# Last layer of a sparse graph network: narrow gathered tiles in float16, multiplied into 32 or 64 rows in three bfloat16 parts

## The chip, the cores and the metric

The kernel runs on 1 core of one Trainium2 chip. The metric is the device time of one launch in microseconds (us). Several runs of one kernel are made on the same chip, and their median is what is compared.

## The reference, cut to what matters

Four layers work on `x` (2708 nodes, 512 features, float32) and a matrix `adj` (2708 x 2708). `adj` is sparse: an entry lies at row i and column j with a chance that falls as both numbers grow, so that the first rows and columns are dense and most of the rest is empty; the diagonal is always there. Every layer ends in `x = layernorm(x + layer(x))`. The change concerns the last one only:

```python
bw = sign(weight)
ba = maximum(sign(x), 0.0)
xw = ba @ bw.T              # whole numbers, at most 512 in size
x = layernorm(x + relu(adj @ xw))
```

The entries of `xw` are whole numbers up to 512 in size, which float16 holds exactly. `adj` is float32 with full mantissas.

## The kernel before

**Blocks and tiles.** The function `sparse_layers` does all the work; `dense_layers` is a fallback for an `adj` with more entries than the lists have room for, and isn't run with this input. The 2708 rows are cut into 22 blocks of 128 (the last has 20). Ahead of the layers the kernel lists for each block b the nodes whose column has an entry in its rows, and packs those columns, transposed, into `packed[b]`: tiles of 128 nodes by 128 rows, float32, which stay in SBUF for all layers. `DIRECT` (L34) names the blocks that take column block 0, or 0 and 1, as whole tiles of their own ("direct"); every other tile of a block is gathered, `ROOM[b]` (L31) of them. In blocks 5 to 21, which this change concerns, there are 70 gathered tiles and 14 direct ones. The diagonal stands apart in `dia_own`.

**Narrow tiles.** The lists are sorted so that the first gathered tiles of a block are narrow (`SPLIT` and `SPANS`, L39 to L46): all entries of such a tile's nodes lie in one quarter of the rows (32 rows, four such tiles, blocks marked QQ) or in one half (64 rows, two tiles, HH); QH and HQ have two quarters and a half. Of the 70 tiles 49 are narrow: 28 in the seven QQ blocks 5 to 10 and 12, 12 in the six HH blocks 11, 13, 15, 17, 18 and 20, and 9 in blocks 14, 16 and 19. Layers 0 to 2 use this already: `span(b, i)` (L1326) gives the rows of a tile, `whole_runs` (L1331) groups the tiles that aren't narrow, `narrow_views` (L1343) gives the narrow ones' part of `packed[b]` by width, `in_turns` (L1360) puts the narrow ones last, and `last_of` (L1373) tells which product closes a row range. The last layer of the kernel before doesn't use it: each tile is multiplied into all 128 rows.

**The last layer** (L1984 to the end of `sparse_layers`). The layer before leaves `xw` as float16 rows in DRAM, `xw_rows`, the last product and write at L1929 and L1936. The products take operands in the format F32R, and `halves_of` (L1994) splits an adjacency tile into two such operands: ScalarE casts it to the high part (L1998), VectorE subtracts that to get the low part (L1999), and each tile takes two products that add up in PSUM. `parts` has four such buffers. There are two kinds of blocks:

- Blocks 0 to 4 (`WHOLE3`) are dense and have a PSUM bank each. `whole_tile(j)` (L2060), for j = 0 to 21, loads 128 rows of `xw_rows` (`xs`, L2064), which `widened` (L2004) turns into F32R, and 128 x 640 of the transposed adjacency (`aw`, L2071, 320 KB, four buffers of its own), splits it, and adds ten products (L2075), two to each bank. These blocks can only end once all 22 steps are done.
- Blocks 21 and 5 to 20 (`order3`) are gathered. For each: its own rows (`xo`, L2087) times its diagonal (`dp`, L2095 by ScalarE and L2098 by VectorE, two products, L2103), then two products for each tile (L2114), the tiles in chunks of four (`CH3`). `gather3` (L2048) issues the gathers of a block, one block ahead: `gathered` (L611) has GpSimd fetch 128 rows by a list of node numbers, as F32R, into a pool of 11 buffers (`xg`). Three PSUM banks take turns.

**The order.** Five whole tiles come first (`AHEAD3`), then the gathered blocks, with a whole tile put in after each three gathers due (`FETCHES3`). `finish3` (L2016) closes a block: VectorE takes `relu` and adds x (L2022) and the moments (L2024), two blocks share a reciprocal root (L642 on ScalarE), ScalarE normalises (L2039), and SP's queue writes 128 rows out (L2043). SP's queue also issues the loads of `xs`, `aw` and `xo`. Which instruction comes when on an engine is set ahead of the run by the scheduler of the Tile framework, which reads this program order and its own costs; within an engine the instructions then run in that order, each waiting for its semaphores.

Of the kernel before, what the change touches and what calls it, by code (L numbers as in the profile page):

```python
# [8 lines left out]
F32 = mybir.dt.float32  # L9
F32R = mybir.dt.float32r  # L10
# [9 lines left out]
P = 128  # L20
# [487 lines left out]
def sparse_layers(ctx, tc, x, adj, adj_t, w0_t, b0, w_sa, a_sa, w_gcnb, b_gcnb, wa, ba, wb, bb, w3_t,  # L508
# [19 lines left out]
    def rows(b: int) -> int:  # L528
        return min(P, N - b * P)

    def direct(b: int):

        return tuple(range(NB)) if b == 0 else DIRECT.get(b, ())

    def tiles(b: int) -> int:
        return len(direct(b)) + ROOM[b]
# [71 lines left out]
    def own_by_itself(b: int) -> bool:  # L608
        return b not in direct(b)

    def gathered(pool, dst_w: int, src, b: int, i: int, dtype=F32):  # L611
        t = pool.tile([P, dst_w], dtype, tag="xg", name=f"xg{b}_{i}")
        nc.gpsimd.indirect_dma_start(  # L613
            out=t, out_offset=None, in_=src[:, :],
            in_offset=bass.IndirectOffsetOnAxis(ap=index[b][:, i : i + 1], axis=0),
        )
        return t
# [708 lines left out]
    def span(b: int, i: int):  # L1326

        t, spans = i - len(direct(b)), SPANS[SPLIT[b]]
        return spans[t][1:] if 0 <= t < len(spans) else (0, rows(b))
# [30 lines left out]
    def in_turns(b: int):  # L1360

        nd, n = len(direct(b)), narrow(b)
        mine = list(range(nd, nd + n))
        return [i for i in range(tiles(b)) if i not in mine] + mine
# [8 lines left out]
    def last_of(b: int, i: int, order):  # L1373

        r0, r1 = span(b, i)
        return all(
            span(b, j)[1] <= r0 or span(b, j)[0] >= r1 for j in order[order.index(i) + 1 :]
        )
# [608 lines left out]
    with tc.tile_pool(name="s_l3", bufs=11, reuse_waits="tile") as lp, \  # L1987
            tc.tile_pool(name="s_ps_w", bufs=1, reuse_waits="tile", space=PSUM) as ps_w, \
            tc.tile_pool(name="s_ps_3", bufs=3, reuse_waits="tile", space=PSUM) as ps_3:
        W3 = WHOLE3 * P  # L1990
        CH3 = 4
        PW = max(CH3 * P, W3)

        def halves_of(a, r: int, w: int, name: str):  # L1994

            p = lp.tile([P, 2, PW], F32R, tag="parts", name=f"p{name}", bufs=4)
            low, high = p[:r, 0, :w], p[:r, 1, :w]
            nc.scalar.copy(high, a)  # L1998
            nc.vector.tensor_tensor(low, a, high.bitcast(F32), op=ALU.subtract)  # L1999
            return p  # L2000

        turn = [0]

        def widened(t, r: int, name: str, tag: str = "wide", bufs: int = 4):  # L2004

            g = lp.tile([P, D], F32R, tag=tag, name=f"w{name}", bufs=bufs)
            turn[0] += 1
            if turn[0] % 3 == 0:
                nc.vector.tensor_copy(g[:r], t[:r])
            else:  # L2010
                nc.scalar.copy(g[:r], t[:r])
            return g

        moments = []

        def finish3(b: int, ps, more: bool):  # L2016

            m = rows(b)
            old = place_of_x(b)
            k = len(moments)  # L2020
            t = old[:, :D]
            nc.vector.scalar_tensor_tensor(t[:m], ps[:m], 0.0, t[:m], op0=ALU.max, op1=ALU.add)  # L2022
            st = small.tile([P, 6], F32, tag="st", name=f"st_3_{b}")
            nc.vector.bn_stats(st[:m], t[:m])  # L2024
            mv = moments[0][2] if k else lp.tile([P, 2, 2], F32, tag="mv3", name=f"mv_3_{b}", bufs=3)
            nc.vector.bn_aggr(mv[:m, k, :], st[:m])
            moments.append((b, t, mv))
            if more:
                return
            n = len(moments)  # L2030
            rs = lp.tile([P, 2, 2], F32, tag="rs3", name=f"rs_3_{b}", bufs=2)
            mean, v = mv[:m, :n, 0], mv[:m, :n, 1]
            nc.vector.tensor_scalar(v, v, LN_EPS, None, op0=ALU.add)
            rsqrt_of(rs[:m, 0, :n], v, m, n, f"3_{b}")
            nc.vector.scalar_tensor_tensor(
                rs[:m, 1, :n], mean, -1.0, rs[:m, 0, :n], op0=ALU.mult, op1=ALU.mult
            )
            for k, (b, t, _) in enumerate(moments):
                nc.scalar.activation(  # L2039
                    t[:m], t[:m], AF.Identity, bias=rs[:m, 1, k : k + 1],  # L2040
                    scale=rs[:m, 0, k : k + 1],
                )
                nc.sync.dma_start(out[b * P : b * P + m, :], t[:m])  # L2043
            moments.clear()

        sources3 = {}

        def gather3(b: int):  # L2048
            sources3[b] = [gathered(lp, D, xw_rows, b, t, F32R) for t in range(ROOM[b])]

        order3 = [NB - 1, *range(WHOLE3, NB - 1)]
        gather3(order3[0])
        gather3(order3[1])


        whole = [ps_w.tile([P, D], F32, tag=f"w{b}", name=f"l3_{b}") for b in range(WHOLE3)]

        xw_direct = {0: xw0}

        def whole_tile(j: int):  # L2060
            r = rows(j)
            if j:
                g = lp.tile([P, D], F16, tag="xs", name=f"xs{j}", bufs=4)
                nc.sync.dma_start(g[:r], xw_rows[j * P : j * P + r, :])  # L2064
                g = widened(g, r, f"s{j}", "wide" if j > 1 else "wide1", 4 if j > 1 else 1)
                if j == 1:
                    xw_direct[1] = g
            else:
                g = xw0
            a = lp.tile([P, W3], F32, tag="aw", name=f"aw{j}", bufs=4)  # L2070
            nc.sync.dma_start(a[:r], adj_t[j * P : j * P + r, :W3])  # L2071
            p = halves_of(a[:r], r, W3, f"w{j}")
            for b in range(WHOLE3):
                for h in range(2):
                    nc.tensor.matmul(  # L2075
                        whole[b], p[:r, h, b * P : (b + 1) * P], g[:r, :],
                        start=(j == 0 and h == 0), stop=(j == NB - 1 and h == 1),
                    )
        j = 0
        while j < AHEAD3:  # L2080
            whole_tile(j)
            j += 1
        due = 0
        for at, b in enumerate(order3):
            m = rows(b)
            xo = lp.tile([P, D], F16, tag="xo", name=f"xo{b}", bufs=2)
            nc.sync.dma_start(xo[:m], xw_rows[b * P : b * P + m, :])  # L2087
            xo = widened(xo, m, f"o{b}")
            if at + 1 < len(order3) and at:
                gather3(order3[at + 1])  # L2090
            src = [xw_direct[j] for j in direct(b)] + sources3.pop(b)
            ps = ps_3.tile([P, D], F32, tag="mm", name=f"l3_{b}")

            dp = lp.tile([P, 2, P], F32R, tag="dp", name=f"dp{b}", bufs=2)
            nc.scalar.activation(  # L2095
                dp[:m, 1, :m], ident[:m, :m], AF.Copy, scale=dia_own[:m, b : b + 1]
            )
            nc.vector.scalar_tensor_tensor(  # L2098
                dp[:m, 0, :m], ident[:m, :m], dia_own[:m, b : b + 1],
                dp[:m, 1, :m].bitcast(F32), op0=ALU.mult, op1=ALU.subtract,  # L2100
            )
            for h in range(2):
                nc.tensor.matmul(  # L2103
                    ps[:m], dp[:m, h, :m], xo[:m, :], start=(h == 0), stop=False
                )
            for i0 in range(0, tiles(b), CH3):
                n = min(CH3, tiles(b) - i0)
                p = halves_of(
                    packed[b][:, i0 : i0 + n, :].rearrange("p n i -> p (n i)"), P, n * m,
                    f"{b}_{i0}",  # L2110
                )
                for i in range(n):
                    for h in range(2):
                        nc.tensor.matmul(  # L2114
                            ps[:m], p[:, h, i * m : (i + 1) * m], src[i0 + i],
                            start=False, stop=(i0 + i == len(src) - 1 and h == 1),
                        )
            pending = bool(moments)
            finish3(b, ps, not pending and b not in (order3[0], order3[-1]))
            if j == NB and whole and len(moments) == 1:  # L2120
                finish3(WHOLE3 - len(whole), whole.pop(0), False)
            due += ROOM[b]
            while j < NB and due >= FETCHES3:
                whole_tile(j)
                j += 1
                due -= FETCHES3
        while whole:
            finish3(WHOLE3 - len(whole), whole.pop(0), len(whole) % 2 == 1)
# [77 lines left out]
```

## Time and profile before

| | |
|---|---|
| Median of three runs | 1006.92 us (1006.87 to 1007.9) |
| Own time of the profiled execution | 1015.66 us |
| Its span | 1013.9 us, 12803 instructions |
| Granted TensorE clock, mean | 0.924 |
| Busy: PE, DVE, ACT, POOL | 867.5, 654.6, 381.2, 513.0 us |
| All transfers | 220.06 MB, mean 217 GB/s |
| Gathers of the whole kernel (queue q0) | 127.61 MB, 42.1% of 16 DMA engines |
| Gathers of the last layer (from 887 us on) | 18.35 MB in 10080 packets |

PE is TensorE's matrix product and PEld its load of weights, which lies beside it; DVE is VectorE, ACT ScalarE, POOL GpSimd, SP the engine whose queue issues most plain transfers. A group of instructions in the profile has its code line, its engine and operation, output<-input by name, shape and count, then its busy time, the mean of one in nanoseconds, and the idle time of the engine ahead of it with what ended most of it. A row of the table of stretches has start and end, length, then the busy time and count of each engine, the granted TensorE clock, the share of the 16 DMA engines that was busy (packets that overlap count each, so it can pass 1) and the GB/s. A row of the chain of waits has the time at which a piece began, its length, and what it was. Averages over the whole kernel say little here: the last layer is one eighth of the span.

### The profile page before, as it was taken

To read this page: it belongs to the slowest core of one execution; us is meant where nothing else is said; L and a number is where in the kernel's file an instruction comes from. 1 tells how busy PE (TensorE), PEld (TensorE's weight loads), DVE (VectorE), ACT (ScalarE), POOL (GpSimd) and SP (SyncE) were. 2 spreads that over 40 slices of the span, in tenths; PEclk is the share of its full clock that TensorE was granted. 3 is DMA by queue.
4 is the path that set the end of the run, shared out by engine and by line. 5 is a ranking of instruction groups with operands and counts; after the bars stand their busy time and mean duration, and the time that the engine had idled before them with its cause. 6 is when DMAs were issued, how large, how long until landed. Compare 5 with 4: busy or idle time off the path is not lost.

```text
span 1013.9 us, 12803 instructions
## 1 busy us (share of the span) xinstructions
PE 867.5 (86%) x3659; PEld 458.7 (45%) x3659; DVE 654.6 (65%) x2538; ACT 381.2 (38%) x822; POOL 513.0 (51%) x579
## 2 busy tenths in 40 slices
PE   1888889659587977989999988998999999699983
PEld 0444444212122324455555544453555555378762
DVE  5889797717366863546455436666888777556765
ACT  2665555100000012545445433333444333254654
POOL 2677888567666533646434034453454320066761
PEclk9898889879798988999999998999999999889986
DMA  9999895467676634766645266676786551299985
GB/s 288 332 330 313 293 299 162 142 197 215 189 228 202 199 122 132 216 198 207 199 150 165 80 235 239 225 272 219 261 320 224 176 176 44 82 308 331 310 233 169
DMA packets 93557, 220.06 MB, mean 217 GB/s; under 512 B 13660, under 2 KB 28364, under 8 KB 93476
## 3 DMA queue, kind: packets, MB, share of 16 engines
q0 software_dynamic: 43008, 127.61, 42.1%
q1 hardware_dynamic: 38520, 76.78, 22.3%
q10 hardware_dynamic: 11948, 14.76, 4.4%
q8 instruction: 31, 0.51, 0.2%
q14 instruction: 50, 0.41, 0.1%
HBM read 178.21 MB, written 31.71 MB: 207 GB/s over the span
## 4 chain that ended last, share of the span: by engine, by line
PE 63%; DVE 15%; issue 6%; DMA 6%; another core or an unknown queue 5%; ACT 3%; POOL 1%; ACTq 0%; DVEq 0%; SPq 0%; POOLq 0%
PE l L1369 11%; PE h L1595 7%; PE e L1820 6%; PE a L1820 6%; PE l L2075 4%; PE y L1106 4%; PE pg L1868 4%; PE l L2114 3%; PE pc L1868 3%; DMA xg<-x_rows,i 2%; PE e L1628 2%; PE px L1929 2%; PE a L1629 2%; DVE s_mask L874 1%
## 5 line engine op out<-in xcount | busy, mean ns | idle before, releaser
L613 POOL DMA_INDIRECT xg<-x_rows,i x98 | 94.8, 967 | 113.4 <-PE l L1369 65.7
L1072 POOL DMA_INDIRECT a<-in_adj_t_dram,row_at x98 | 111.0, 1132 | 59.2 <-DVE deg L817 24.0
L613 POOL DMA_INDIRECT xg<-y_rows,i x98 | 97.5, 995 | 50.3 <-issue 21.8
L1106 PE MATMUL y<-s_w,xt 128*128 128x512 f32 (+1 forms) x176 | 96.8, 702 | 0.0
L1369 PE MATMUL l<-xg,a 128*32 128x512 f32 (+3 forms) x196 | 83.2, 657 | 12.1 <-DMA xg<-y_rows,i 11.8
L613 POOL DMA_INDIRECT xg<-xw_rows,i x70 | 71.4, 1020 | 39.9 <-issue 16.5
L1796 POOL DMA_INDIRECT xg<-x_rows,i x60 | 59.9, 999 | 61.8 <-ACT ae L1551 18.0
L1595 PE MATMUL h<-s_wsa,xt 128*128 128x256 f32 (+3 forms) x352 | 83.5, 391 | 5.2 <-ACT xt L1590 5.0
L1796 POOL DMA_INDIRECT a<-x_rows,i x38 | 36.9, 970 | 93.3 <-DVE mask L1554 38.0
L1595 PEld LDWEIGHTS h<-s_wsa,xt 128*128 128x128 f32 (+1 forms) x352 | 65.4, 190 | 30.6 <-ACT xt L1590 14.0
L809 ACT ACTIVATE unused<-arow 128x1408 uint8<-128x1408 f32 (+3 forms) x44 | 58.3, 1325 | 2.4 <-DMA x_rows<-s_zero 1.7
L1106 PEld LDWEIGHTS y<-s_w,xt 128*128 128x128 f32 (+1 forms) x176 | 37.3, 223 | 43.4 <-issue 43.3
L2075 PE MATMUL l<-ws,pw 128*128 128x512 f32 (+1 forms) x210 | 52.0, 401 | 3.7 <-DVE pw L1999 3.7
L1820 PE MATMUL a<-xg,a 128*32 128x512 f32 (+2 forms) x120 | 50.9, 626 | 4.2 <-DMA xg<-x_rows,i 4.2
L1820 PE MATMUL e<-xg,ae 128*32 128x512 f32 (+2 forms) x120 | 47.9, 601 | 0.9 <-ACT ae L1556 0.9
L642 ACT ACTIVATE rsqs<-mv 128x1 f32<-128x1 f32 (+2 forms) x56 | 11.3, 201 | 94.8 <-DVE mv L671 48.9
L2075 PEld LDWEIGHTS l<-ws,pw 128*128 128x128 f32 (+1 forms) x210 | 40.4, 194 | 14.0 <-DVE pw L1999 4.6
L1868 PE MATMUL pg<-s_wg,pt 128*128 128x256 f32 (+1 forms) x176 | 44.9, 397 | 1.3 <-ACT pt L1856 1.3
L895 PE MATMUL find<-s_sides,s_mask 128*128 128x5 bf16 (+1 forms) x462 | 15.7, 166 | 34.8 <-DVE s_mask L891 25.0
L667 DVE BATCH_NORM_STATS2 st<-t 128x6 f32<-128x512 f32 (+1 forms) x66 | 45.3, 686 | 0.3
L1369 PEld LDWEIGHTS l<-xg,a 128*32 128x32 f32 (+3 forms) x196 | 19.6, 148 | 53.2 <-issue 33.0
L673 POOL TENSOR_TENSOR rs<-mv,s_neg_half 128x1 f32<-128x1 f32 (+1 forms) x22 | 12.9, 588 | 60.5 <-DVE mv L671 51.1
(306 smaller groups left out, 1965.6 us busy)
## 6 DMA issues: line engine op xcount, KB each, us to landing
arow<-in_adj_dram SPq DMA_DIRECT2D x21, 704.0 KB
arow<-in_adj_dram SPq DMA_DIRECT2D x21, 650.0 KB
x_rows<-f SPq DMA_DIRECT2D x40, 256.0 KB
aw<-in_adj_t_dram SPq DMA_DIRECT2D x21, 320.0 KB
y_rows<-yt ACTq DMA_DIRECT2D x20, 256.0 KB
x_rows<-h SPq DMA_DIRECT2D x19, 257.0 KB
f<-in_x_dram SPq DMA_DIRECT2D x19, 256.0 KB
h_own<-x_rows SPq DMA_DIRECT2D x19, 256.0 KB
```

The costliest lines, as they stand in the source:

```text
L613: nc.gpsimd.indirect_dma_start(out=t, out_offset=None, in_=src[:, :], in_offset=bass.IndirectOffsetOnAxis(ap=index[b][:, i : i + 1], axis=0),)
L667: nc.vector.bn_stats(st[:m], t[:m])
L809: nc.scalar.activation(unused[:m, : ar.shape[1]], ar, AF.Copy, accum_out=row_sums[:m, b, h : h + 1])
L1072: nc.gpsimd.indirect_dma_start(out=packed[b][:, t + len(direct(b)), :], out_offset=None, in_=adj_t, in_offset=bass.IndirectOffsetOnAxis(ap ...
L1106: nc.tensor.matmul(ps[:m], xt[:, k, :m], w0[:, k, :], start=(k == 0), stop=(k == KC - 1))
L1369: nc.tensor.matmul(ps[r0:r1], weights, moving, start=(i == order[0]), stop=last_of(b, i, order))
L1595: nc.tensor.matmul(ps, xt[:, k, :m], w[:, k, :], start=(k == 0), stop=(k == KC - 1))
L1796: nc.gpsimd.indirect_dma_start(out=g, out_offset=None, in_=x2_rows[:, :], in_offset=bass.IndirectOffsetOnAxis(ap=index[b][:, t : t + 1], a ...
L1820: nc.tensor.matmul(ps[r0:r1], weights, moving, start=(i == order[0]), stop=last_of(b, i, order))
L1868: nc.tensor.matmul(ps, pt[:, k, :m], w[:, k, :], start=(k == 0), stop=(k == KC - 1))
L2075: nc.tensor.matmul(whole[b], p[:r, h, b * P : (b + 1) * P], g[:r, :], start=(j == 0 and h == 0), stop=(j == NB - 1 and h == 1),)
L2114: nc.tensor.matmul(ps[:m], p[:, h, i * m : (i + 1) * m], src[i0 + i], start=False, stop=(i0 + i == len(src) - 1 and h == 1),)
```

## The change

The narrow tiles of the last layer are treated as such, as in the layers before:

- `gather3` fetches a narrow tile's 128 rows as float16, as they lie in DRAM, into buffers of their own (`xh`, 12), and a whole tile's as F32R as before (`xg`, 8); of one block the whole tiles are fetched first, the narrow ones last.
- To make room, the tiles of adjacency streamed for blocks 0 to 4 (`aw`) have no buffers of their own: they take turns in four slices of `packed[1]`, `packed[2]` and `packed[3]`, which the last layer doesn't read.
- Whole tiles are split in two and multiplied as before, but in the runs that `whole_runs` gives.
- A narrow block's part of the adjacency is split in three bfloat16 parts (`thirds`, two buffers, with the float32 rest in `left`, one buffer): ScalarE copies the high part of the block's 32- or 64-row pieces, VectorE subtracts it, ScalarE copies the middle part, VectorE subtracts again. Where a block has quarters and a half (14, 16, 19), the first two steps are made once for each width.
- Each narrow tile then takes three products, high part first, each into its own 32 or 64 rows of the block's PSUM bank: all tiles of the block with one part, then with the next.

```diff
--- before.py
+++ after.py
@@ -608,8 +608,8 @@
     def own_by_itself(b: int) -> bool:
         return b not in direct(b)
 
-    def gathered(pool, dst_w: int, src, b: int, i: int, dtype=F32):
-        t = pool.tile([P, dst_w], dtype, tag="xg", name=f"xg{b}_{i}")
+    def gathered(pool, dst_w: int, src, b: int, i: int, dtype=F32, tag="xg", bufs=None):
+        t = pool.tile([P, dst_w], dtype, tag=tag, name=f"{tag}{b}_{i}", bufs=bufs)
         nc.gpsimd.indirect_dma_start(
             out=t, out_offset=None, in_=src[:, :],
             in_offset=bass.IndirectOffsetOnAxis(ap=index[b][:, i : i + 1], axis=0),
@@ -2046,7 +2046,14 @@
         sources3 = {}
 
         def gather3(b: int):
-            sources3[b] = [gathered(lp, D, xw_rows, b, t, F32R) for t in range(ROOM[b])]
+            nd = len(direct(b))
+            sources3[b] = {
+                i: gathered(
+                    lp, D, xw_rows, b, i - nd, *((F16, "xh", 12) if span(b, i) != (0, rows(b))
+                    else (F32R, "xg", 8)),
+                )
+                for i in in_turns(b) if i >= nd
+            }
 
         order3 = [NB - 1, *range(WHOLE3, NB - 1)]
         gather3(order3[0])
@@ -2056,6 +2063,11 @@
         whole = [ps_w.tile([P, D], F32, tag=f"w{b}", name=f"l3_{b}") for b in range(WHOLE3)]
 
         xw_direct = {0: xw0}
+
+        streamed = [
+            packed[b].rearrange("p n i -> p (n i)")[:, k * W3 : (k + 1) * W3]
+            for b, k in ((1, 0), (2, 0), (1, 1), (3, 0))
+        ]
 
         def whole_tile(j: int):
             r = rows(j)
@@ -2067,7 +2079,7 @@
                     xw_direct[1] = g
             else:
                 g = xw0
-            a = lp.tile([P, W3], F32, tag="aw", name=f"aw{j}", bufs=4)
+            a = streamed[j % 4]
             nc.sync.dma_start(a[:r], adj_t[j * P : j * P + r, :W3])
             p = halves_of(a[:r], r, W3, f"w{j}")
             for b in range(WHOLE3):
@@ -2088,7 +2100,9 @@
             xo = widened(xo, m, f"o{b}")
             if at + 1 < len(order3) and at:
                 gather3(order3[at + 1])
-            src = [xw_direct[j] for j in direct(b)] + sources3.pop(b)
+            src = sources3.pop(b)
+            src.update((i, xw_direct[c]) for i, c in enumerate(direct(b)))
+            order_ = in_turns(b)
             ps = ps_3.tile([P, D], F32, tag="mm", name=f"l3_{b}")
 
             dp = lp.tile([P, 2, P], F32R, tag="dp", name=f"dp{b}", bufs=2)
@@ -2103,8 +2117,7 @@
                 nc.tensor.matmul(
                     ps[:m], dp[:m, h, :m], xo[:m, :], start=(h == 0), stop=False
                 )
-            for i0 in range(0, tiles(b), CH3):
-                n = min(CH3, tiles(b) - i0)
+            for i0, n in whole_runs(b, CH3):
                 p = halves_of(
                     packed[b][:, i0 : i0 + n, :].rearrange("p n i -> p (n i)"), P, n * m,
                     f"{b}_{i0}",
@@ -2113,7 +2126,28 @@
                     for h in range(2):
                         nc.tensor.matmul(
                             ps[:m], p[:, h, i * m : (i + 1) * m], src[i0 + i],
-                            start=False, stop=(i0 + i == len(src) - 1 and h == 1),
+                            start=False, stop=h == 1 and last_of(b, i0 + i, order_),
+                        )
+            if narrow(b):
+                p = lp.tile([P, 3, P], BF16, tag="thirds", name=f"p{b}_n", bufs=2)
+                left = lp.tile([P, P], F32, tag="left", name=f"r{b}", bufs=1)
+                mine = []
+                for i0, r0, w, a in narrow_views(b):
+                    n = a.shape[1]
+                    nc.scalar.copy(p[:, 2, r0 : r0 + n * w].rearrange("p (n i) -> p n i", n=n), a)
+                    nc.vector.tensor_tensor(
+                        left[:, r0 : r0 + n * w].rearrange("p (n i) -> p n i", n=n), a,
+                        p[:, 2, r0 : r0 + n * w].rearrange("p (n i) -> p n i", n=n),
+                        op=ALU.subtract,
+                    )
+                    mine += range(i0, i0 + n)
+                nc.scalar.copy(p[:, 1, :], left)
+                nc.vector.tensor_tensor(p[:, 0, :], left, p[:, 1, :], op=ALU.subtract)
+                for h in (2, 1, 0):
+                    for i in mine:
+                        r0, r1 = span(b, i)
+                        nc.tensor.matmul(
+                            ps[r0:r1], p[:, h, r0:r1], src[i], start=False, stop=h == 0
                         )
             pending = bool(moments)
             finish3(b, ps, not pending and b not in (order3[0], order3[-1]))
```

In the changed file the lines are: gathers L613 as before, `streamed` L2067, loads of `xs` L2076, of `aw` L2083 and of `xo` L2099, products of whole tiles of blocks 0 to 4 L2087, of the diagonal L2117, of gathered whole tiles L2127; the narrow blocks' four steps L2137 (ACT), L2138 (DVE), L2144 (ACT), L2145 (DVE), and their products L2149.

## The prediction

> **What bounds the kernel now.** I read the page's 40 slices first, then the last layer alone: its groups of instructions, its busy time by stretch, and the chain of waits. The layer runs from the first gather at 889.05 us to the end of the span. Its groups:
>
> ```profile
> L613 POOL DMA_INDIRECT xg<-xw_rows,i x70 | 71.4, 1020 | 39.9 <-issue 16.5 <-PE l L2114 8.4 <-DMA xw_rows<-xw 7.6
> L2075 PE MATMUL l<-ws,pw 128*128 128x512 f32 (+1 forms) x210 | 52.0, 401 | 3.7 <-DVE pw L1999 3.7
> L2114 PE MATMUL l<-xg,p 128*128 128x512 f32 (+1 forms) x140 | 37.3, 412 | 0.0
> ```
>
> The gathered products (L2114) take 37.3 us of TensorE, and GpSimd waited 8.4 us for them to free gather buffers. The stretches (start and end, length, then busy PE, PEld, DVE, ACT, POOL, then granted clock and DMA share):
>
> ```profile
> 889.00:903.00 14.00, 13.98 (x51) 11.04 (x52) 4.83 (x8) 4.62 (x9) 10.65 (x11) 0.83 1.19 344
> 903.00:969.30 66.30, 65.80 (x286) 52.82 (x284) 45.17 (x116) 38.55 (x76) 46.39 (x45) 1.00 1.10 316
> 969.30:981.80 12.50, 9.29 (x33) 6.93 (x33) 9.17 (x24) 7.27 (x15) 7.48 (x8) 0.86 0.77 216
> 981.80:1002.10 20.30, 16.10 (x55) 12.14 (x54) 15.33 (x59) 10.56 (x21) 6.88 (x8) 0.77 0.66 197
> 1002.10:1013.90 11.80, 0.00 (x0) 0.00 (x0) 4.34 (x20) 2.75 (x6) 0.00 (x0) 0.50 0.38 141
> ```
>
> Until 969.3 TensorE is the bound, with the DMA engines also full (share over 1, as packets overlap). Then it starves once. 981.8 is the end of the last whole tile (L2075), after which five waiting blocks can be finished; the 20.3 us from there to the last matmul belong mostly to VectorE (15.3 busy). The chain says where TensorE starved:
>
> ```profile
> 966.49 4.39 issue
> 970.87 0.73 ACT pw L1998
> 971.63 0.84 DVE pw L1999
> 972.51 4.05 PE l L2075 x10
> ```
>
> "issue" ahead of the cast of an adjacency tile means that ScalarE waited for something the profile doesn't show; with the DMA full I read it as the tile's late load. TensorE then restarts at a low clock: 4.05 us for ten products that take 2.27 in the chain at 944.69. So a product of 128x512 costs 0.227 us.
>
> **What the Trainium skill says.** "TensorEngine Tiling (Array Packing)", Tiling Modes: 32-column weights make four independent tiles, 64-column ones two, and changing the mode drains the array. The trace agrees for float32 in layer 1:
>
> ```profile
> 498.64 0.82 PE L1595 MATMUL h<-s_wsa,xt 128*128 128x260 f32 x3
> 499.39 1.07 PE L1369 MATMUL l<-xg,incn 128*32 128x512 f32 x8
> 500.38 0.70 PE L1628 MATMUL e<-h,e 128*128 128x512 f32 x1
> ```
>
> Eight passes over four 32-row tiles fit before 500.38, while full tiles need 0.86 us for two passes (483.29 to 484.15): four run side by side. The next full product starts 0.13 us after 499.39 + 0.86; where a narrow one follows a full one (535.47 + 0.86, then 536.42) it is 0.09. I price a change of mode at 0.11. "TensorE: Matmul & The Clock Gate", Measured speedup vs the span model, gives 2.38x for three column tiles, less than this trace; that is my lower bound. Its Back-to-back issue gap gives 215.7 ns for 512 columns; the bfloat16 px products here (L1929) take 0.86 for four, 0.215. "DMA: Bandwidth & Descriptors", SWDGE vs HWDGE vs iDMA, says a float32r destination always casts. In the trace a float16 row does land as 2 KB: 18.35 MB in 70 gathers is 128 rows of 2 KB each.
>
> **The change part by part.** The built program shows the order on each engine; durations are from the trace.
>
> 1. Narrow products. 49 of the 70 gathered tiles are narrow. Gone: 98 products x 0.227 = 22.2 us. Added: blocks of one width (7 of four tiles, 6 of two) need 3 rounds each, the three mixed ones (14, 16, 19) 6, since 32 and 64 columns alternate: (39 + 18) x 0.227 = 12.9. Changes of mode: 13 x 2 + 3 x 7 = 47, x 0.11 = 5.2. TensorE net: -4.1. What counts is the part before the last whole tile, blocks 5 to 15: 37 tiles, 74 x 0.227 = 16.8 gone, 36 rounds = 8.2 and 27 changes = 3.0 added: -5.6. After it, 5.4 gone and 4.8 + 2.2 added: +1.6 on TensorE, beside a VectorE that is slower there; 0 on the path, 1.6 without that cover. Bounds of the overlap: all of it (this), 2.38 of 4 (0.38 us a round of four, +3.2 before the last whole tile), none (rival B).
> 2. Start. The two dp steps (0.31 and 0.40 before the cast at 887.40) stand behind the first cast now: -0.65.
> 3. Streamed tiles in the place of blocks 1 to 3. The first four loads move ahead of SP's h_own loads of blocks 19 and 20. They wait for the last reads of block 18's rows (the product at 841.61); h_own 19 waits for u at 843.09 anyway and is used at 855.07. Cost 0; uncovered, 11 us of slack would have to go first. The load itself (1.3 MB) falls where no gather is in flight (830 to 889). Later loads still wait only for their own reader, four back.
> 4. DMA. A 2-KB packet takes 108 ns (queue q0: 53.5% of 16 engines over 126.9 us, 10080 packets); the 1-KB rows written by queue q10 take 42 ns. I take 54, half (bounds 42 and 108). 35 narrow gathers fall before 970: each saves 128 x 54 ns / 16 = 0.43, in all 15 of the 89.6 share-us up to 969.3 (14.0 x 1.19 + 66.3 x 1.10). That is 17%, more than TensorE's speed-up of 5.6 in 92, so I take the starvation as gone: 3.2 of wait (969.3 to 972.5) and 1.8 of slow clock, -5.0. Bound: 0, if the wait isn't the DMA's.
> 5. Gathers. 20 buffers end GpSimd's 12 us of waits for TensorE, but the order moves: xg of later blocks goes ahead, and block 8's last narrow gather becomes the 26th. At 1.245 us each (0.94 + 0.30) it is issued at 889.05 + 25 x 1.245 + 0.94 = 921.1; with about 2 us to land (an estimate from the fixed cost that the same DMA page gives under Anatomy of one DMA; no run here shows it), 923.1, against a need near 922: +1, between 0 and 2.4 (mean pace 1.32). The 70th lands at 978 to 984, before TensorE needs it.
> 6. Preparation. Casts and subtractions of whole tiles: 20 of 128 columns (0.29), 7 of 256 (0.40 on ScalarE, 0.41 on VectorE), one small: 8.8 us on each engine. Narrow ones: 35 steps x 0.29 = 10.1 on each. Against 14.4 (ACT) and 15.6 (DVE) now: +4.5 and +3.3. Beside TensorE, which has the longer queue; but a narrow block is a chain of four steps over two engines (1.2 us), with one `left` and two `thirds` buffers, and behind it in both queues stand casts of streamed tiles. I book +1 (0 to 4).
> 7. The tail. 20.3 us from last whole tile to last matmul, set by VectorE, and 11.8 after it: unchanged (17 to 22 for the first).
>
> Sum: -5.6 - 0.65 - 5.0 + 1 + 1 = -9.2 us. The profiled execution's own time is 1015.66 (span 1013.9 and 1.8 around it), 8.7 above the median of the runs, 1006.92; scaling by their ratio changes the 9.2 by 0.1, so I subtract it: 997.7.
>
> **Rivals.**
> A. Preparation or late loads keep TensorE waiting: the wait at 969 stays (-5.0 lost) and the chain of step 6 costs 2 more: -9.2 + 5.0 + 2 = -2.2, 1004.7. For it: VectorE and ScalarE gain work. Against: 45.2 and 38.6 busy of 66.3.
> B. Slower: 16-bit narrow products do not run side by side. 111 products x 0.227 + 3.0 - 16.8 = +11.4 before the last whole tile, -0.65 - 5.0 + 2: +7.8, 1014.7. It decides from 0.157 us a product ((16.8 - 3.0 + 5.65 - 2) / 111), fewer than 1.45 side by side. Against it: float32 shows four.
> C. The tail shrinks too: VectorE waited 4.7 us there for products (L2022 on L2114), and nothing of steps 5 and 6 shows: 17 for 20.3, -9.2 - 3.3 - 2 = -14.5, 992.4.
> D. It does not do what it says: the saved TensorE time lies in the shadow of the gathers (70 x 1.32 = 92 us) and nothing changes: 1006.9.
>
> **Numbers.** Forecast 0.47, A 0.22, C 0.20, B 0.07, D 0.04. A measurement of this kernel tells 0.2% (2 us) from no change. Faster: 0.47 + 0.20 + nearly all of A = 0.87; same 0.05; slower 0.08. Range 989.5 to 1005: from 3 below C (tail at its lower bound, casts cheaper) to A; it leaves out B, D and some of A.
>
> **What would show it.** Step 1: narrow groups of 128*32 with twelve products in about 0.7 us. Step 4: DMA share below 1.0 from 903 on, no gap ahead of a streamed cast near the end. Step 5: GpSimd without waits for PE, last gather by 982. Steps 1 to 6 together: last whole tile near 972.6; step 7: 20 us from there to the last matmul. I am wrong if rounds take over 0.4 us, or if TensorE waits for thirds or casts by more than 3 us in all.

## The result and the profile after

The changed kernel took 1019.26 us (median of six runs, 1017.22 to 1029.47), the kernel before on the same chip 1007.63. The ratio is 1.0118, with a 95% interval of 1.0084 to 1.0153: slower by 1.2%, where 0.9% faster was forecast, and outside the range. A ratio is worked out from the single runs, without those in a slower state of the chip, and so need not be the quotient of the medians. The profiled execution took 1018.41 us, span 1016.1.

The first layers ended earlier in this profile than in the one of before (last write of `xw_rows` issued at 879.16 against 886.41), so only the last layer is compared, counted from that write. Until the end of the span it took 137.0 us against 127.5.

Groups of the last layer, to be held against L2075 and L2114 of before:

```profile
L2087 PE MATMUL l<-ws,pw 128*128 128x512 f32 (+1 forms) x210 | 57.4, 428 | 14.3 <-issue 10.3 <-DVE rsqs L661 2.3 <-DVE pw L1999 1.7
L613 POOL DMA_INDIRECT xh<-xw_rows,i x49 | 49.1, 1003 | 23.8 <-issue 11.3 <-remote 3.6 <-PE l L2149 3.5
...
L2149 PE MATMUL l<-xh,p_n 128*32 128x512 f16 (+1 forms) x147 | 17.9, 386 | 1.7 <-ACT p_n L2144 1.6
...
L2022 DVE SCALAR_TENSOR_TENSOR f<-l,f 128x512 f32<-128x512 f32 (+1 forms) x20 | 13.7, 689 | 21.0 <-remote 10.1 <-PE l L2127 3.6 <-PE l L2149 3.2
```

TensorE idled 14.3 us ahead of products of streamed tiles, 3.7 before. VectorE waited 10.1 us in the first step of `finish3` for a signal ("remote") that the profile can't pin to an instruction that ended just then. A signal is an update of a semaphore, by which one engine tells the others that an instruction of its own is done. The stretches:

```profile
881.40:898.70 17.30, 17.23 (x74) 12.61 (x74) 6.16 (x15) 6.65 (x17) 13.10 (x13) 0.88 0.91 279
898.70:912.70 14.00, 7.38 (x20) 5.46 (x20) 4.01 (x9) 3.92 (x8) 8.50 (x9) 0.76 0.73 206
912.70:986.20 73.50, 64.64 (x314) 43.93 (x312) 47.86 (x153) 42.24 (x104) 48.15 (x49) 0.95 0.74 223
986.20:1004.10 17.90, 14.88 (x66) 7.12 (x66) 15.32 (x65) 10.11 (x28) 0.00 (x0) 1.00 0.29 107
```

The DMA share fell from 1.10 to about 0.74, as forecast, and bought nothing. In the second row everything stands half idle: 7.4 us of TensorE, 4 of VectorE and ScalarE in 14 us. The timeline of TensorE there, then of VectorE (start, length, and in brackets the idle time before):

```profile
897.85 0.83 PE L2149 MATMUL l<-xh,p_n 128*32 128x512 f16 x12
903.98 5.93 PE L2087 MATMUL l<-ws,pw 128*128 128x512 f32 x14 [5.30 <-issue]
910.93 0.39 PE L2087 MATMUL l<-ws,pw 128*128 128x512 f32 x1 [1.01 <-issue]
```

```profile
902.52 0.68 DVE L2022 SCALAR_TENSOR_TENSOR f<-l,f 20x512 f32<-20x512 f32 x1 [2.39 <-remote]
903.12 0.80 DVE L1999 TENSOR_TENSOR pw<-a,pw 128x640 fp32r<-128x640 f32 x1
...
911.94 0.69 DVE L2022 SCALAR_TENSOR_TENSOR f<-l,f 128x512 f32<-128x512 f32 x1 [6.60 <-remote]
```

The `f` at 911.94 is block 5's; in the built program it waits for TensorE alone, for block 5's last narrow product. That product ended at 898.7, so its signal came 13 us late. The `f` at 902.52 is block 21's, whose last product ended at 896.1: 6 us late. In VectorE's queue the subtraction of the next streamed tile (903.12) stands behind it, and TensorE waits for that from 898.7 to 903.98. Then it runs fourteen products in 5.93 us, at half clock.

The kernel before had this too. In its trace the updates of TensorE's semaphore have times: 85 of the 663 that were recorded came more than 0.6 us after any product that makes one had ended, and one of them, at 970.81, is what released the cast at 970.87: before it, the trace has no update of that semaphore after 961.58, though TensorE ended products up to 969.26. The cast's wait covers two semaphores, TensorE's and that of its own load, and the load, issued at 948.95, had its last packet at 953.77. The "issue" before that cast, which the prediction read as a late load, was a late signal.

### The profile page after: what moved, and what is told of

Same layout as the page of the kernel before. It is cut to its first block, busy times and chain, and to the rows that moved or that the text cites. A ratio compares the mean times of both kernels' runs of the same rounds, so it can differ in the third digit from the quotient of the medians.

```text
span 1016.1 us, 12953 instructions
## 1 busy us (share of the span) xinstructions
PE 860.2 (85%) x3708; PEld 442.5 (44%) x3708; DVE 652.3 (64%) x2571; ACT 383.5 (38%) x855; POOL 512.2 (50%) x579
## 4 chain that ended last, share of the span: by engine, by line
PE 61%; DVE 14%; issue 7%; DMA 6%; another core or an unknown queue 4%; ACT 3%; POOL 3%; ACTq 0%; DVEq 0%; SPq 0%; POOLq 0%
PE l L1369 12%; PE h L1595 7%; PE e L1820 6%; PE a L1820 6%; PE l L2087 5%; PE pg L1868 3%; PE y L1106 3%; PE pc L1868 3%; POOL xg L613 2%; DMA xg<-x_rows,i 2%; PE e L1628 2%; DVE s_mask L874 2%; PE a L1629 2%; PE l L1430 2%
## 5 line engine op out<-in xcount | busy, mean ns | idle before, releaser
L613 POOL DMA_INDIRECT xg<-x_rows,i x98 | 94.8, 968 | 109.6 <-PE l L1369 62.2
L613 POOL DMA_INDIRECT xg<-y_rows,i x98 | 98.7, 1007 | 45.5 <-issue 22.5
L1106 PE MATMUL y<-s_w,xt 128*128 128x512 f32 (+1 forms) x176 | 92.4, 674 | 1.8 <-ACT xt L1098 1.8
L1796 POOL DMA_INDIRECT xg<-x_rows,i x60 | 59.7, 995 | 63.0 <-ACT ae L1551 17.7
L2087 PE MATMUL l<-ws,pw 128*128 128x512 f32 (+1 forms) x210 | 57.4, 428 | 14.3 <-issue 10.3
L613 POOL DMA_INDIRECT xh<-xw_rows,i x49 | 49.1, 1003 | 23.8 <-issue 11.3
L2087 PEld LDWEIGHTS l<-ws,pw 128*128 128x128 f32 (+1 forms) x210 | 42.3, 206 | 29.0 <-issue 13.5
L1369 PEld LDWEIGHTS l<-xg,a 128*32 128x32 f32 (+3 forms) x196 | 20.3, 150 | 55.8 <-issue 35.9
L874 DVE TENSOR_SCALAR s_mask<-arow 128x1408 bf16<-128x1408 f32 (+3 forms) x42 | 39.6, 942 | 5.6 <-DMA arow<-in_adj_dram 5.6
```

Source lines behind the costliest of these rows:

```text
L613: nc.gpsimd.indirect_dma_start(out=t, out_offset=None, in_=src[:, :], in_offset=bass.IndirectOffsetOnAxis(ap=index[b][:, i : i + 1], axis=0),)
L874: nc.vector.tensor_scalar(mask[:m, c0 : c0 + ar.shape[1]], ar, 0.0, None, op0=ALU.not_equal)
L1106: nc.tensor.matmul(ps[:m], xt[:, k, :m], w0[:, k, :], start=(k == 0), stop=(k == KC - 1))
L1369: nc.tensor.matmul(ps[r0:r1], weights, moving, start=(i == order[0]), stop=last_of(b, i, order))
L1796: nc.gpsimd.indirect_dma_start(out=g, out_offset=None, in_=x2_rows[:, :], in_offset=bass.IndirectOffsetOnAxis(ap=index[b][:, t : t + 1], a ...
L2087: nc.tensor.matmul(whole[b], p[:r, h, b * P : (b + 1) * P], g[:r, :], start=(j == 0 and h == 0), stop=(j == NB - 1 and h == 1),)
```

## The experiments

There were six sets of runs: the recorded one and five more, each set on one chip together with the kernel before. They found two levels, and the trace tells them apart:

| | Chip number on record | Kernel before, median | Late updates of TensorE's semaphore, before or nearest kernel |
|---|---|---|---|
| Recorded runs | none | 1007.63 | 85 of 663 in the trace (796 were due) |
| Set 1 | 7 | 1010.73 | 88 of 663 (room18) |
| Set 2 | 15 | 960.12 | 3 of 796 (again) |
| Set 3 | 9 | 960.56 | 3 of 809 (changed) |
| Set 4 | 1 | 1020.15 | 135 of 680 (onering2) |
| Set 5 | 7 | 959.97 | 3 of 801 (stream11b) |

So the signals are late and partly missing in the trace at one level, prompt and complete at the other, and the kernel before is 47 to 60 us faster where they are prompt. That they make up the whole of this difference isn't shown: the last layer's part of it is 9.3 us in the profiles (127.5 against 118.2 in `again`). Nor is it known what makes them late. Sets 1 and 5 have the same chip number and different levels, so, if the number stands for one piece, it isn't the chip alone; whether the taking of the trace has a part no run here can tell. The ratios against before, with their intervals:

| Kernel | Late signals | Prompt signals |
|---|---|---|
| changed | 1.0118 [1.0084, 1.0153] | 1.0024 [1.0009, 1.0039] |
| slices alone (not run with late signals) | | 0.9994 [0.9971, 1.0017]; 0.9999 [0.9977, 1.0020] |
| slices, 18 buffers | 1.0094 [1.0057, 1.0131] | 0.9992 [0.9974, 1.0010] |
| apart | 1.0141 [1.0088, 1.0194] | |
| plain32 | 1.0073 [1.0040, 1.0107] | |
| halves16 | 1.0105 [1.0061, 1.0149] | |
| ownaw | | 1.0047 [1.0029, 1.0066] |
| few | | 1.0024 [1.0005, 1.0043]; 1.0042 [1.0026, 1.0057] |
| onering | 1.0068 [1.0044, 1.0092] | 0.9952 [0.9930, 0.9974] |
| ring16 | 1.0012 [0.9980, 1.0043] | |
| ringplain | 1.0020 [0.9989, 1.0051] | |
| all16 (not run with late signals) | | 0.9934 [0.9908, 0.9959]; 0.9930 [0.9912, 0.9949] |

The theories before set 1, in the letters of the expectations: P, the narrow tiles' preparation keeps TensorE waiting; S, its signals are late because narrow products come in dense bursts; B, the slices or the new buffers cost. From set 2 on, S stands for the slices alone and G for gathers that run ahead and crowd other loads; from set 3 on, O for the order of gathers and L for late signals.

**Set 1: one part alone, and less preparation.** `room18` is the kernel before with the slices and 18 buffers:

```diff
-    with tc.tile_pool(name="s_l3", bufs=11, reuse_waits="tile") as lp, \
+    with tc.tile_pool(name="s_l3", bufs=18, reuse_waits="tile") as lp, \
...
+        streamed = [
+            packed[b].rearrange("p n i -> p (n i)")[:, k * W3 : (k + 1) * W3]
+            for b, k in ((1, 0), (2, 0), (1, 1), (3, 0))
+        ]
...
-            a = lp.tile([P, W3], F32, tag="aw", name=f"aw{j}", bufs=4)
+            a = streamed[j % 4]
```

> The kernel before with the buffers alone changed: streamed adjacency tiles in the slices of packed[1..3], 18 gather buffers for 11, all tiles still whole, F32R, in the old order of gathers. Theory P (the narrow blocks' four steps of preparation and the ring of `parts` keep TensorE waiting): same as before within 0.3%, or up to 4 us faster, since GpSimd waits less. Theory S (TensorE's completion signals come late because narrow products are issued in dense bursts): the same, 1003 to 1008. Theory B (it is the streamed slices or the new buffers): slower than before by 5 us or more, 1012 to 1019.

Measured 1018.10, the loss that theory B expected, without one narrow tile.

`apart` is the changed kernel with the split parts of the gathered blocks' whole tiles in buffers apart (`own` is true for these):

```diff
-            p = lp.tile([P, 2, PW], F32R, tag="parts", name=f"p{name}", bufs=4)
+            own = w < W3
+            p = lp.tile(
+                [P, 2, 2 * P if own else W3], F32R, tag="few" if own else "parts",
+                name=f"p{name}", bufs=3 if own else 4,
+            )
```

> The changed kernel, with the split parts of gathered whole tiles in three buffers of their own (256 columns), so that the four `parts` buffers belong to the streamed tiles alone and their casts can run further ahead. Theory P: 4 to 10 us faster than the changed kernel, 1009 to 1015. Theories S and B: within 2 us of it, 1017 to 1021.

Measured 1021.97: no gain, so sharing the ring of `parts` isn't the cause.

`plain32` multiplies narrow tiles in float32, gathered as float32 into 9 buffers, without any preparation (the lines that fall away aren't shown):

```diff
-                    lp, D, xw_rows, b, i - nd, *((F16, "xh", 12) if span(b, i) != (0, rows(b))
+                    lp, D, xw_rows, b, i - nd, *((F32, "xh", 9) if span(b, i) != (0, rows(b))
...
+                for i in range(len(direct(b)), len(direct(b)) + narrow(b)):
+                    r0, r1 = span(b, i)
+                    nc.tensor.matmul(
+                        ps[r0:r1], packed[b][:, i, r0:r1], src[i], start=False, stop=True
+                    )
```

> The changed kernel, with the narrow tiles multiplied in plain float32 straight from packed[b] (two passes in one instruction, as layer 1 does) on rows gathered as float32: no thirds, no left, none of the four steps on ScalarE and VectorE; 9 narrow buffers for 12. TensorE has about 0.2 us more for a QQ block, and gathered rows land as 2 KB again. Theory P: most of the loss is gone, 1004 to 1011. Theory S: the bursts stay, 1016 to 1021. Theory B: 1017 or more, as the packets are larger too.

Measured 1019.75, where theories S and B expected it and P didn't; its runs spread from 1011.82 to 1029.71.

`halves16` uses two float16 parts:

```diff
-                p = lp.tile([P, 3, P], BF16, tag="thirds", name=f"p{b}_n", bufs=2)
+                p = lp.tile([P, 2, P], F16, tag="halves", name=f"p{b}_n", bufs=4)
...
-                for h in (2, 1, 0):
+                for h in (1, 0):
```

> The changed kernel, with two float16 parts for three bfloat16 ones of each narrow tile: two steps of preparation for four, two rounds of products for three, four buffers for the parts. Theory P: half of the loss or more is gone, 1005 to 1013. Theory S: bursts are shorter (8 for 12 products), 1013 to 1018. Theory B: 1016 to 1019, TensorE's saved rounds at most.

Measured 1019.09. Theory P (preparation) had expected gains of 4 us or more from all of the last three. The changed kernel itself wasn't in this set; against its recorded ratio of 1.0118 theirs are 1.0141, 1.0073 and 1.0105, and all the intervals overlap. P in that size fell, S didn't fit `room18`, and theory B was left.

**Set 2: which half of theory B.** `stream11` is `room18` with 11 buffers.

> The kernel before with one edit: streamed adjacency tiles in the slices of packed[1..3]; 11 gather buffers, whole tiles, F32R. Theory S (the streamed slices cost: their first loads go ahead of others on SP's queue, and the casts come in another order): slower than before by 5 to 10 us. Theory G (gathers that run ahead of TensorE crowd the loads of streamed tiles and own rows): within 2 us of before.

`ownaw` is the changed kernel with `aw` in its own buffers and 9 `xh`.

> The changed kernel with the streamed tiles in four buffers of their own again; to make room, 9 narrow gather buffers for 12. Theory S: most of the loss is gone, 1000 to 1010. Theory G: 17 buffers let the gathers run ahead as before, 1015 to 1020.

`few` is the changed kernel with 5 `xg` and 6 `xh` buffers.

> The changed kernel with 5 buffers for whole gathered tiles and 6 for narrow ones, 11 in all as in the kernel before; streamed slices as changed. Theory S: no gain, 1016 to 1021. Theory G: GpSimd is held back again and the loss is mostly gone, 1005 to 1011.

`again` is the kernel before.

> The kernel before, unchanged, for a second profile of it and for the spread of its own times. Every theory: the same time; from the last write of xw_rows to the end of the span some 127 us, as in the first profile, with one gap of TensorE before the last whole tile.

Measured 961.10, 965.38, 963.78 and 960.54 against 960.12. The slices cost nothing here, so theory S fell for this level, and `ownaw` kept a loss without them. `few` kept one too, with 11 buffers, so theory G found no support. But the level was new, so that the times expected can't be held against these, and `again` showed why; its groups and its stretch up to the last whole tile:

```profile
L2075 PE MATMUL l<-ws,pw 128*128 128x512 f32 (+1 forms) x210 | 49.7, 390 | 0.0
...
L2114 PE MATMUL l<-xg,p 128*128 128x512 f32 (+1 forms) x140 | 35.9, 401 | 0.0
```

```profile
842.50:928.40 85.90, 85.90 (x369) 69.51 (x369) 60.01 (x148) 51.72 (x100) 63.41 (x63) 0.98 1.16 331
```

TensorE doesn't wait at all, with the DMA share even higher, at 1.16. The expectation of one gap was wrong: with prompt signals there is no starvation to cure.

**Set 3: the changed kernel with prompt signals, and its gathers put in order.** `changed` is the changed kernel.

> The changed kernel once more, unaltered, because the chips so far differ in level (the kernel before took 1007 to 1011 us on the first, 960 us on the second, where TensorE's completion signals were hardly ever late). Theory O (two rings of buffers let the whole gathered tiles of later blocks overtake the narrow ones, and TensorE waits near block 8) and theory L (late signals on some chips, which hit the changed kernel more): slower than before by 0.2 to 0.6% where signals are prompt, with a wait of 3 to 6 us on a narrow gather near the 23rd to 26th; slower by 1.0 to 1.4% where they are late. If it is slower by 1% with prompt signals, both fall.

Measured 962.28 against 960.56, and the wait was where theory O put it. TensorE and then GpSimd near block 8:

```profile
878.32 0.39 PE L2149 MATMUL l<-xh,p_n 128*32 128x512 f16 x1
879.57 0.38 PE L2149 MATMUL l<-xh,p_n 128*32 128x512 f16 x1 [0.86 <-DMA xh<-xw_rows,i]
880.54 0.38 PE L2149 MATMUL l<-xh,p_n 128*32 128x512 f16 x1 [0.59 <-DMA xh<-xw_rows,i]
881.60 0.81 PE L2149 MATMUL l<-xh,p_n 128*32 128x512 f16 x9 [0.68 <-DMA xh<-xw_rows,i]
```

```profile
867.75 1.04 POOL L613 DMA_INDIRECT xg<-xw_rows,i  x1 [0.30 <-issue]
869.10 0.94 POOL L613 DMA_INDIRECT xg<-xw_rows,i  x1 [0.30 <-issue]
870.34 0.94 POOL L613 DMA_INDIRECT xg<-xw_rows,i  x1 [0.30 <-PE l L2087]
871.58 1.44 POOL L613 DMA_INDIRECT xg<-xw_rows,i  x1 [0.30 <-issue]
873.33 0.95 POOL L613 DMA_INDIRECT xh<-xw_rows,i  x1 [0.30 <-PE l L2127]
...
877.36 0.95 POOL L613 DMA_INDIRECT xh<-xw_rows,i  x1 [0.30 <-PE l L2087]
```

Four gathers into free `xg` buffers, whole ones of blocks 9 to 11, go ahead of block 8's four into `xh`; the fourth of these is issued at 877.36, and TensorE, there since 878.32, goes on at 881.60.

`onering` gives both kinds one ring, of 14 buffers of 2 KB, the same space (a second edit, not shown, makes a float16 tile's buffer 2 KB too):

```diff
-                    lp, D, xw_rows, b, i - nd, *((F16, "xh", 12) if span(b, i) != (0, rows(b))
-                    else (F32R, "xg", 8)),
+                    lp, D, xw_rows, b, i - nd, F16 if span(b, i) != (0, rows(b)) else F32R, "xg", 14,
```

> The changed kernel with one ring of 14 buffers of 2 KB for both kinds of gathered tiles, so that gathers are issued block by block; all else as changed. Theory O: the wait near block 8 is gone, 3 to 6 us faster than the changed kernel on the same chip, equal to before or up to 0.3% faster. Theory L, with late signals: within 2 us of the changed kernel.

Measured 955.21: 7.1 us less than `changed`, 5.4 less than before, both somewhat more than theory O expected. The same place, block 8's narrow products and what follows, then the stretch up to the last whole tile:

```profile
873.21 0.83 PE L2149 MATMUL l<-xg,p_n 128*32 128x512 f16 x12
873.97 4.84 PE L2087 MATMUL l<-ws,pw 128*128 128x512 f32 x20
```

```profile
838.00:919.80 81.80, 81.77 (x406) 58.37 (x406) 59.44 (x176) 52.86 (x127) 62.90 (x61) 0.97 0.90 273
```

81.8 us where the kernel before takes 85.9, and no wait. `room18b` is `room18` again.

> The kernel before with the streamed slices and 18 gather buffers for 11, again, on the chip of these runs. The streamed slices alone cost nothing. Theory G (gathers that run ahead crowd other loads): slower than before by 0.5 to 1.0% on any chip. Theory L: the same as before within 0.2% where signals are prompt, slower by 0.7 to 1.1% where they are late.

Measured 959.62: what cost 0.94% with late signals costs nothing with prompt ones, as theory L expected. Theory G, in its form "on any chip", fell.

`all16` does the whole layer in float16: `halves_of`, `dp` and `xw0` in F16, `widened` gone, narrow tiles in two parts, one ring of 36 gather buffers, and more buffers for `xs`, `xo` and `parts`. Two of its edits:

```diff
-            xo = widened(xo, m, f"o{b}")
...
-            dp = lp.tile([P, 2, P], F32R, tag="dp", name=f"dp{b}", bufs=2)
+            dp = lp.tile([P, 2, P], F16, tag="dp", name=f"dp{b}", bufs=2)
```

> The whole last layer in float16: every adjacency tile in two float16 parts, rows of xw used as they lie (no casts of xs and xo), all gathers float16 in one ring of 36 buffers, narrow tiles in two rounds, six buffers for parts, streamed slices. It takes 38 casts of 0.4 to 0.6 us from ScalarE and VectorE, and a third of the narrow rounds. Theory O: GpSimd's pace (70 x 1.245 us) is left as the bound, and the time falls by 5 to 10 us against before. Theory L with late signals: a gain of 0 to 5 us, since fewer steps stand between TensorE and its next tile.

Measured 954.96, the lowest median, though not apart from that of `onering`; which of its parts does it wasn't separated. Its groups show what is next; the narrow products wait 6.3 us for gathers:

```profile
L613 POOL DMA_INDIRECT xg<-xw_rows,i x70 | 72.5, 1036 | 28.6 <-issue 14.6 <-DMA xw_rows<-xw 7.5 <-DMA xg<-xw_rows,i 1.5
...
L2130 PE MATMUL l<-xg,p_n 128*32 128x512 f16 (+1 forms) x98 | 16.0, 406 | 6.4 <-DMA xg<-xw_rows,i 6.3
```

**Set 4: late signals again.** `onering2` is `onering`; `ring16` and `ringplain` are `halves16` and `plain32` with its ring.

> The changed kernel with one ring of 14 buffers, again. With prompt signals: 0.3 to 0.7% faster than before, as it was. With late signals (the kernel before then takes 1005 to 1012 us): theory L, that they and not the order of gathers made the recorded loss, expects 0.5 to 1.2% slower than before; theory O alone expects 0 to 0.7% faster there too.

> One ring of 14 buffers, and the narrow tiles in two float16 parts for three bfloat16 ones: two steps of preparation for four, two rounds for three. TensorE saves one round of 0.2 us for each of 13 blocks and more for the mixed three. If the four steps (theory P) cost anything on the path once the order is mended: 3 to 6 us faster than with three parts; if only rounds count: 1.5 to 3 us faster.

> One ring of 14 buffers, and the narrow tiles in plain float32 straight from packed[b], on rows gathered as float32: no preparation of narrow tiles at all, some 0.2 us more of TensorE for each block, larger packets. Theory P: faster than three parts by 2 us or more. If the preparation was hidden: slower than three parts by 1 to 4 us.

Measured 1025.07, 1021.29 and 1024.34 against 1020.15. The kernel that gains 0.5% with prompt signals loses 0.7% with late ones, as theory L expected. Here the wait is on signals and not on gathers; TensorE, ScalarE and VectorE of `onering2`:

```profile
907.57 0.83 PE L2149 MATMUL l<-xg,p_n 128*32 128x512 f16 x12
913.92 3.35 PE L2087 MATMUL l<-ws,pw 128*128 128x512 f32 x7 [5.52 <-DVE pw L2000]
```

```profile
912.08 0.72 ACT L1999 CAST pw<-a 128x640 fp32r<-128x640 f32 x1 [7.65 <-remote]
```

```profile
912.12 0.43 DVE L2010 CAST wo<-xo 128x512 fp32r<-128x512 f16 x1 [7.89 <-remote]
```

Two parts for three took 3.8 us off the median. The intervals of the two ratios just fail to meet (1.0044 and 1.0043), so part of this loss seems to go with the three parts; whether by their steps or by their rounds was not separated. 3.8 us is what theory P's steps were expected to be worth (3 to 6), but `ringplain`, which has no such steps at all, can't be told from either.

**Set 5: which part late signals punish.** `stream11b`, `few2` and `all16b` are the kernels of those names.

> The kernel before with the streamed slices alone, 11 buffers, again. With late signals (before at 1005 to 1020 us): if the gathers that run ahead are what makes late signals worse (18 buffers alone cost 0.94% there), within 0.3% of before; if it is the slices, 0.6 to 1.0% slower. With prompt signals: the same as before, as it was.

> The changed kernel with 5 whole and 6 narrow gather buffers, 11 in all, again. With late signals: 0 to 0.5% slower than before if gathers that run ahead make them worse; 1% or more slower if it is the narrow products and their preparation. With prompt signals: 0.1 to 0.4% slower, as it was.

> The last layer all in float16, again. With prompt signals 0.4 to 0.9% faster than before, as it was. With late signals: between 0.5% faster and 0.5% slower; it has the fewest steps between TensorE and its next tile, and the most gathers in flight (36 buffers).

Measured 960.46, 963.77 and 954.29 against 959.97: prompt signals again, so these three repeat what was known, and their question stays open.

## Why the prediction was wrong, step by step

- **What bounds the kernel, and step 4 (-5.0).** This is the step that failed. The one gap before the last whole tile was taken for a load that the full DMA made late, and its end was booked as gained. It was a late signal (970.81, above), and the tile's load had landed 17 us before it ended. With prompt signals there is no gap to remove (`again`), and with late ones the changed kernel has eight gaps of over half a microsecond, 14.8 us in all up to the last whole tile, where before had 3.2; the sum had no term for such waits. Packets did get lighter: with prompt signals, share times length up to the last whole tile is 99.6 us in `again` (1.16 of 85.9) and 77.5 in `changed` (0.89 of 87.1), 22% less where 17% was forecast. So the price was of the right size, and its use was wrong.
- **Step 1 (-5.6).** Right in the mechanism. Twelve products of 32 rows take 0.76 us to the next full one, and 0.10 more at the start; six of 64 rows 0.77. Rounds of four start 0.22 us apart (the bound of 2.38, which is for three tiles, had 0.38). With prompt signals, taken from product to product up to the last whole tile, the gathered tiles take 23.8 us in `again`, and 17.7 in `changed` without the wait at block 8: -6.1. But a cost stood outside this price: the first full product behind a narrow group takes 0.335 us until the next one starts, for 0.227. Eleven groups make that 1.2, so that a group costs 0.97 for the 0.90 forecast, and -4.9 is left.
- **Step 5 (+1, up to 2.4).** The mechanism was right to the place, block 8's last narrow gather as the 26th, and the size was wrong. That group took 4.01 us for 0.76, so the wait was 3.3, and a stretch of 3.4 us at half clock followed it (882.4 to 885.8), 1.7 more: 5.0. The landing took 3.3 us from the end of GpSimd's instruction (878.3 to 881.6), where 2 was taken, and TensorE reached the block (878.32) just as GpSimd ended that gather. That the clock would drop wasn't counted at all. "TensorE: Matmul & The Clock Gate" of the Trainium skill says, under "What's actually happening", that an idle window of about 3.4 us puts TensorE at half clock until a busy one. The traces agree in that half clock comes in steps of 3.4 us, here after waits of 3.3 us within 4, but not in the length of the wait: in the recorded profile a stretch of it (977.6 to 981.0) came after one wait of 1.66 us.
- **Step 2 (-0.65).** The first product came 2.28 us after the last write for 2.61, half of what was booked.
- **Step 3 (0).** Right with prompt signals: the slices alone are at 0.9994 and 0.9999. With late ones they were run only together with more gather buffers (`room18` and the changed kernels).
- **Step 6 (+1, up to 4).** With prompt signals TensorE waits for the thirds only in the tail, 1.6 us. With late signals the four steps may be worth some of the 3.8 us between `onering2` and `ring16`.
- **Step 7 (unchanged).** Last whole tile to last matmul: 17.9 for 20.3 in the recorded profile, and 19.4 for 17.8 with prompt signals, where a half-clock stretch (930.2 to 933.6) and those 1.6 us fall into it. The profile of `stream11`, without narrow products, has such a stretch (930.0 to 933.4) and 19.4 us too, so this need not be the change's.

With prompt signals the sum is about -4.9 - 0.3 + 5.0 + 1.5 for the tail and 0.4 after it: +1.7, where the profiles differ by 2.8 from the last write to the end. The rest, about 1 us, is that the half clock after the start lasted until 7.8 us after the last write for 5.9. In the recorded runs, by contrast, the waits are what counts. From the last write to the last whole tile the layer took 107.0 us for 95.4, while TensorE's gaps grew by 11.6 and its half clock after the start by 10.2 us, worth 5.1. Less 4.9 for the narrow products, that is 11.8, near the 11.6 by which the stretch grew.

Of the rivals only A, "preparation or late loads keep TensorE waiting", had TensorE wait; it was given 1004.7, since it held the wait at 969 for the only one. B's number, 1014.7, came nearest by luck: its mechanism was wrong, as the 16-bit products do run four side by side.

What stays open: which part of the change makes late signals cost more. Gathers that run ahead can't be excluded, nor the slices (`room18`, with both and no narrow tile, lost 0.94%), nor the three parts. Nor is it known what delays the signals. No version that was run where they are late beats before; `ring16` came nearest (1.0012), and `all16` wasn't run there.

## What to carry to other kernels

A buffer pool split by kind also splits the order of what fills it: the kind with free room overtakes, and the consumer waits for the other. Keep one ring, or issue by due time, when one engine issues both. And before a gap is booked as gained, look up which semaphore ended it and when, and when the load that is blamed had landed: here a gap that looked like a late load was a signal of TensorE, and it wasn't the change's to remove.

## What was not expected of the hardware

One kernel ran at 960 us in some sets and at 1007 to 1020 in others, at a mean granted clock of 0.952 and 0.924 in the two profiles of the kernel before. At the slow level TensorE's signals came up to 13 us after its products had ended, often several within 0.3 us of each other. A change of half a percent had opposite signs at the two levels (0.9952 and 1.0068).
